# Where the table of x's remainders is made in VectorE's octet: two operations in a row, or one in each of two places

## The chip, the cores and the metric

The kernel runs on one core of a Trainium2 chip. The metric is the device time of one execution in microseconds; of several runs the median is given. The core has five engines with instruction streams of their own: PE (TensorE, matmuls), DVE (VectorE), ACT (ScalarE), POOL (GpSimd) and SP (SyncE, which here only issues DMAs). They wait for each other through semaphores.

## The reference

One layer of a graph network with 12500 nodes (x: 12500 x 64) and 400000 edges, sorted by their destination, with 16 attributes each. For every edge a small network works on the rows of its two nodes and on its attributes, the messages are added up by destination, and a node's row and its sum make the new row:

```python
m_in = jnp.concatenate([x[src], x[dst], edge_attr], axis=-1)
h = jax.nn.silu(m_in @ W1 + b1)
messages = jax.nn.silu(h @ W2 + b2)
agg = jax.ops.segment_sum(messages, dst, num_segments=x.shape[0])
node_in = jnp.concatenate([x, agg], axis=-1)
out = jax.nn.silu(node_in @ W3 + b3)
x = _layernorm(x + out, axis=-1)
```

## The kernel before

**Octets.** The edges are cut into 3125 tiles of 128 and these into 391 octets of up to 8 tiles. One turn of the main loop (`for o in range(NO + 2)`) works on several octets at once: it compares the destinations of octet o + 2 (`compare_nodes`, L587), turns octet o + 1 (L605 on PE, L615 on VectorE), runs the first layer of octet o (L640, L643, L644 on PE, the activation h at L647 on ACT), the second layer of octet o - 2 (L656 and L658 on PE, the activation m at L662 on ACT), the sum of octet o - 4 (L671 on PE) and its addition into the table `agg` at octet o - 5 (`add_window`, L682 on VectorE). An h activation happens once an octet.

**Where an edge's source row comes from.** The 8 tiles are 4 pairs. Most pairs are gathered by GpSimd with an indirect DMA for each tile (L538, tile `ga`), up to octet 10 from x and from octet 11 on from `pa`, the product of x with a part of W1. These gathers stand in no order with the other engines: GpSimd goes on until the ring of five `ga` buffers is full, and then waits for the PE transposes (L640) that read the oldest. Other pairs are picked from the resident transposed x, a node's column after another: by ACT (L447, tile `cx`), by VectorE (L449, `cx`), by PE (`pick`, tile `pg`), and by single DMAs from SP (`rx`).

**Columns.** `columns(o, engine, part)` copies a share of such columns. On VectorE a part is 0 or 32 edges, 16 instructions of L449, and ahead of it stands a TENSOR_LOAD (L430) that reads the 32 addresses into registers. Part 1 is empty; part 3 is empty in three octets of seven.

**The table of remainders.** PE's pick is exact in float32 up to octet 57 (L396). From octet 58 it adds two bfloat16 products instead (L400 and L402): the upper halves of x's float32 words, and the remainders, x minus its upper halves, from the table `rest2`. `remainders(k)` makes that table on VectorE, 512 columns in four operations: k % 4 = 0 subtracts for the lower 64 partitions (L810, into `rest2`), 1 subtracts for the upper 64 (L812, into a buffer in `v`), 2 casts that buffer into `rest2` (L814), 3 subtracts the rounded value from it (L816). L814 reads what L812 wrote, and L816 what L814 wrote. There are 100 operations in all. The same memory had served before as a staging buffer for `pa` (L232 and its DMAs, up to octet 6).

**The order of the work.** Instructions of PE, ACT, VectorE and SP stand in the order in which this loop is written (`manual_schedule`). On VectorE an octet is: L682, L587, the remainders, columns part 0 (L430, L449), `window_copy` (L567), L615, columns part 2, columns part 3 where there is one, now and then node work (L732, L737, L738, L750), address arithmetic (L523), limits (L288). L615 frees the one PSUM buffer `ph` into which PE's next L605 writes, so PE's turn of octet o + 2 waits for L615 of octet o + 1.

Of the kernel before, what the change touches and what calls it, by code (L numbers as in the profile page):

```python
# [32 lines left out]
BEGIN = 4  # L33
# [29 lines left out]
def kernel(  # L63
# [51 lines left out]
    with ExitStack() as inner:  # L115
        flag = windows(inner, tc, ident, identb, twice, badi, pa, x, xt, xt2, src_c, src_row, src_pair, dst_c, dst_row, attr_t, attr_2, base, w1, b1, w2, b2, w3, b3, out, edges)
# [5 lines left out]
def windows(ctx, tc, ident, identb, twice, badi, pa, x, xt, xt2, src_c, src_row, src_pair, dst_c, dst_row, attr_t, attr_2, base, w1, b1, w2, b2, w3, b3, out, edges):  # L122
# [5 lines left out]
    NO = base.shape[1]  # L128
# [184 lines left out]
    with tc.tile_pool(name="gat", bufs=AHEAD + 2) as gat, \  # L313
# [20 lines left out]
        def shares(eng, o):  # L334
            if o < BEGIN:
                return (0, 0, 0, 0)
            if eng == ENG.Activation:
                return ACOLS if (o - BEGIN) % 7 % 3 < 2 else (ACOLS[0] - 16, ACOLS[1])
            n = (o + 1 - BEGIN) * VRATE[0] // VRATE[1] - (o - BEGIN) * VRATE[0] // VRATE[1]
            return VCOLS if n == 3 else VCOLS[:3] + (0,)  # L340
# [75 lines left out]
        def columns(o, eng, part):  # L416
            if o < BEGIN:
                return
            lo = counts[eng][o] + sum(shares(eng, o)[:part])
            hi, most = lo + shares(eng, o)[part], LOADS[eng == ENG.DVE]  # L420
            while lo < hi:
                j, e0 = lo // (2 * P), lo % (2 * P)
                if j >= len(pairs[eng]):
                    return
                n = min(hi - lo, 2 * P - e0, most)
                key = eng, pairs[eng][j]
                if key not in cols:
                    cols[key] = cx.tile([P, P], F32, name="cx")
                t = cols[key].bitcast(U8)
                _, regs = nc.values_load_multi_w_load_instructions(  # L430
                    indices[eng, j][0:1, e0:e0 + n], engines=(eng,), min_val=XADDR,
                    max_val=X2ADDR + 4 * (N - 1), skip_runtime_bounds_check_because="src names a node")

                def at(i, u, a):
                    return u[:, ds(regs[i].with_bounds(min_val=a, max_val=a + 4 * (N - 1)) - a, 4)]

                def word(i, u, a):
                    o = (regs[i] - a).with_bounds(min_val=0, max_val=4 * (N - 1), guaranteed_mod_val=0, out_of_modulus=4)
                    return u[:, ds(o, 4)].bitcast(F32)

                for i in range(n):
                    e = e0 + i
                    if e % 8 >= 4:
                        continue
                    k = e // 8 * 4 + e % 4
                    if eng == ENG.Activation:
                        nc.scalar.activation(cols[key][:, k:k + 1], word(i, xb, XADDR), AF.Identity, bias=word(i + 4, x2b, X2ADDR))  # L447
                    else:
                        nc.vector.tensor_tensor(t[:, 4 * k:4 * k + 4], at(i, xb, XADDR), at(i + 4, x2b, X2ADDR), op=OP.max)  # L449
                lo += n  # L450
# [109 lines left out]
        def window_product(o):  # L560
            pw = mis.tile([P, P], F32, name="mm")
            nc.tensor.matmul(pw[:E, :], winrow[o], w1bb.rearrange("k s m -> k (s m)"),  # L562
                             start=True, stop=True)
            winrow[o] = pw

        def window_copy(o):
            nc.vector.tensor_tensor(xw[o % 3][:E, :], winrow.pop(o)[:E, :], mask[:E, :], op=OP.mult)  # L567
# [11 lines left out]
        def compare_nodes(o):  # L579
            c, t0, n, first, last = octs[o]  # L580
            eh = ehp.tile([P, OT // 2, S, 2], F32, name="eh")
            rel = dcs[t0 // SCT].bitcast(F32)
            t0 = t0 % SCT

            def compare(i, k, s, w):
                at = t0 + 2 * i + s
                nc.vector.tensor_tensor(eh[:, i:i + k, :, s:s + w], row[:, None, :, None].to_broadcast([P, k, S, w]),  # L587
                                        rel[:, at:at + k * w].rearrange("p (i s) -> p i s", s=w)[:, :, None, :].to_broadcast([P, k, S, w]),
                                        op=OP.is_equal)

            k = n // 2
            compare(0, k, 0, 2)
            if n % 2:
                compare(k, 1, 0, 1)
                nc.vector.memset(eh[:, k, :, 1], 0.0)
            hots[o] = [eh]
# [12 lines left out]
        def turned(o):  # L609
            c, t0, n, first, last = octs[o]  # L610
            eh, ph = hots[o]
            e = o % 3 * OT // 2 * P
            w = (n + n % 2) // 2 * P
            oh = loaded[c][:, e:e + w]
            nc.vector.tensor_copy(oh[:E, :], ph[:E, :(n + 1) // 2].rearrange("p i e -> p (i e)"))  # L615
            hots[o] = oh, eh
# [155 lines left out]
        for q in range(rest):  # L772
            o = lead[due[q]] + LAST - 1
# [11 lines left out]
        for q0, q1 in batches:  # L785
            o = lead[due[q1 - 1]] + LAST + 2 * G
# [10 lines left out]
        def remainders(k):  # L797

            c = k // 4 * RW
            if c >= N:  # L800
                return
            w = min(RW, N - c)
            at = slice(c, c + w)

            def top(t):
                return t.bitcast(BF16).rearrange("p (n s) -> p n s", s=2)[:, at, 1]

            left = v[D:, 2 * RB - 2:].rearrange("p a i d -> p (a i d)")[:, :w]
            if k % 4 == 0:
                nc.vector.tensor_tensor(rest2[:D, at], xs[:D, at], top(xs)[:D], op=OP.subtract)  # L810
            elif k % 4 == 1:
                nc.vector.tensor_tensor(left, x2[D:, at], top(x2)[D:], op=OP.subtract)  # L812
            elif k % 4 == 2:
                nc.vector.tensor_copy(rest2[D:, at], left)  # L814
            else:
                nc.vector.tensor_tensor(rest2[D:, at], left, rest2[D:, at], op=OP.subtract)  # L816
# [52 lines left out]
        with tc.manual_schedule(engines={ENG.PE, ENG.Activation, ENG.DVE, ENG.SP}):  # L869
# [8 lines left out]
            for o in range(NO + 2):  # L878
# [50 lines left out]
                        nc.vector.memset(t[:, c:min(c + XC, w)], 0.0)  # L929
                if o + 2 < NO:  # L930
                    compare_nodes(o + 2)
                for k in (2 * (o - BEGIN - 5), 2 * (o - BEGIN - 5) + 1) if o >= BEGIN + 5 else ():
                    remainders(k)
                columns(o, ENG.DVE, 0)
                def behind():
                    for q in adds.get(o, []):
# [18 lines left out]
                if o + 1 < NO:  # L955
                    if o + 1 < NO - 1:
                        window_copy(o + 1)
                    if o + 1 == NO - 2:
                        window_product(o + 2)
                        window_copy(o + 2)  # L960
                    columns(o, ENG.DVE, 1)
                    turned(o + 1)
                    columns(o, ENG.DVE, 2)
                columns(o, ENG.DVE, 3)
                if phase == 20:
# [317 lines left out]
```

## Time and profile before

| | |
|---|---|
| median of 3 runs | 3247.89 us (3245.48 to 3252.06) |
| the profiled execution, its own time | 3249.99 us |
| its span | 3248.0 us |
| busy: PE / DVE / ACT / POOL | 2642.2 / 2119.8 / 3084.4 / 2425.1 us |
| gathers from pa (L538) | 2459, 953 ns each in the mean |
| remainders: L810, L812, L814, L816 | 25 each, median 671, 689, 425, 690 ns |
| first and last start of a remainder | 128.8 and 564.1 us |

The span runs from the first to the last instruction of the profiled execution; its own time has the start and the end around it. In groups of instructions, a line names the source line, engine, operation, output and inputs; behind the bar stand busy time, the mean of one in ns, and the engine's idle time just before them with what ended it. "issue" is time in which an engine waited for nothing that the profile shows. A row with "<-" between two instructions is a wait: who waited for whom, us in total, how often, and the longest. A window's row has the engines' busy times PE, PEld (weight loads), DVE, ACT, POOL with instruction counts, then the granted TensorE clock, the DMA share and GB/s. Rows of a timeline have start, duration, and in brackets the idle time before.

### The profile page before, as it was taken

What the parts mean: (1) busy time and instruction counts of PE and PEld (TensorE: products, weight loads), DVE (VectorE), ACT (ScalarE), POOL (GpSimd) and SP (SyncE); (2) the same over time, 40 slices, a digit from 0 to 9 for tenths busy, and PEclk for the clock granted to TensorE, in tenths of its full rate; (3) what the DMA queues carried; (4) which work ended last, traced back from release to release, by engine and by line L of the source; (5) the groups of instructions that cost most, each with busy time, mean ns of one, the idle gap of its engine ahead of it and who ended that gap; (6) DMA issues with size and microseconds to landing.
All of it is one profiled execution on the core that took longest, in us unless ns stands there. A gap on an engine that the chain in (4) does not pass through costs nothing. (4 is left out here: it accounts for less than half of the span.)

```text
span 3248.0 us, 124643 instructions
## 1 busy us (share of the span) xinstructions
PE 2642.2 (81%) x32267; PEld 2170.6 (67%) x32267; DVE 2119.8 (65%) x18208; ACT 3084.4 (95%) x15185; POOL 2425.1 (75%) x2551
## 2 busy tenths in 40 slices
PE   7788778788787887887888888878888778888776
PEld 5677667676676766666666667667666666666664
DVE  5577777666666666666666666666666666666663
ACT  2799988999999999999999999999999999999994
POOL 7777776777777777777777777777777777777775
PEclk8787877787777777878877777877778788777887
DMA  7211111221221221222221222222221221222211
GB/s 148 49 41 40 40 39 37 43 48 42 43 43 41 49 43 43 43 46 44 43 44 41 46 43 43 43 43 46 43 44 41 45 46 42 44 43 45 44 41 36
DMA packets 157997, 148.42 MB, mean 46 GB/s; under 512 B 101606, under 2 KB 111604, under 8 KB 156516
## 3 DMA queue, kind: packets, MB, share of 16 engines
q0 software_dynamic: 81376, 83.49, 13.5%
q1 hardware_dynamic: 61406, 47.11, 5.6%
q10 hardware_dynamic: 14502, 9.75, 1.4%
q8 instruction: 272, 4.46, 0.6%
q14 instruction: 441, 3.61, 0.4%
HBM read 133.72 MB, written 6.40 MB: 43 GB/s over the span
## 5 line engine op out<-in xcount | busy, mean ns | idle before, releaser
L538 POOL DMA_INDIRECT ga<-pa,sc x2459 | 2344.6, 953 | 772.0 <-issue 661.0
L447 ACT ACTIVATE cx<-xs,x 128x1 f32 x14336 | 2829.6, 412 | 18.8 <-issue 14.8
L449 DVE TENSOR_TENSOR cx<-xs,x 128x4 uint8 x15616 | 1261.1, 155 | 1009.4 <-issue 989.8
L658 PEld LDWEIGHTS p<-w2d,h 128*128 128x128 f32 x3126 | 512.7, 233 | 245.9 <-issue 227.9
L402 PEld LDWEIGHTS <-twice 128*128 128x128 bf16 x7680 | 434.8, 100 | 265.5 <-issue 257.2
L400 PEld LDWEIGHTS <-twice 128*128 128x128 bf16 x7680 | 469.6, 100 | 124.6 <-issue 124.6
L644 PE MATMUL p<-oh,xw 128*128 128x512 f32 x760 | 545.9, 811 | 0.0
L400 PE MATMUL pg<-xs,twice 128*128 x7680 | 478.5, 165 | 69.5 <-DVE px L414 35.6
L658 PE MATMUL p<-w2d,h 128*128 128x128 f32 x3126 | 514.5, 319 | 0.0
L402 PE MATMUL pg<-rest,twice 128*128 x7680 | 468.0, 164 | 1.6 <-DVE rest L816 1.6
L605 PE MATMUL ph<-identb,eh 128*96 128x128 bf16 x1563 | 206.6, 271 | 243.2 <-DVE oh L615 237.2
L656 PE MATMUL p<-b2r,one 128*128 128x512 bf16 x391 | 172.6, 441 | 232.3 <-ACT m L662 231.3
L605 PEld LDWEIGHTS <-eh 128*96 128x96 bf16 x1563 | 150.5, 159 | 264.2 <-DVE oh L615 256.1
L647 ACT ACTIVATE h<-p 128x512 f32<-128x512 f32 x391 | 275.4, 704 | 52.6 <-PE p L644 27.1
L662 ACT ACTIVATE m<-p 128x512 f32<-128x512 f32 x391 | 276.0, 706 | 36.7 <-PE p L658 33.5
L671 PE MATMUL pg<-eh,m 128*64 128x48 f32 x6250 | 307.2, 245 | 0.7 <-ACT m L662 0.7
L640 PE MATMUL p<-ident,ga 128*128 128x128 f32 x1230 | 268.5, 344 | 10.6 <-DMA ga<-pa,sc 10.6
L671 PEld LDWEIGHTS pg<-eh,m 128*64 128x64 f32 x6250 | 255.7, 158 | 22.7 <-issue 13.3
L615 DVE COPY oh<-ph 96x512 f32<-96x512 f32 x391 | 263.3, 673 | 2.2 <-PE ph L605 2.1
L587 DVE TENSOR_TENSOR eh<-wrow,dc 128x384 f32<-128x384 f32 x392 | 213.3, 544 | 10.7 <-ACT z L726 6.1
L562 PE MATMUL mm<-w1bb,xr 66*96 66x128 f32 x782 | 214.8, 367 | 0.8 <-ACT rest L232 0.7
L640 PEld LDWEIGHTS p<-ident,ga 128*128 128x128 f32 x1230 | 206.1, 184 | 12.1 <-issue 12.1
(127 smaller groups left out, 1846.8 us busy)
## 6 DMA issues: line engine op xcount, KB each, us to landing
rx<-pa SPq DMA_DIRECT2D x6144, 0.2 KB
ga<-pa,sc POOLq DMA_INDIRECT x2459
oh<-in_attr SPq DMA_DIRECT2D x130, 192.0 KB
xr<-in_xt SPq DMA_DIRECT2D x391, 24.4 KB
cxi<-in_src_pair SPq DMA_DIRECT2D x234, 1.0 KB
xs<-in_xt ACTq DMA_DIRECT2D x6, 512.0 KB
pa<-rest ACTq DMA_DIRECT2D x12, 256.0 KB
x<-in_xt ACTq DMA_DIRECT2D x6, 512.0 KB
```

What stands on the lines that cost most here:

```text
L400: nc.tensor.matmul(g[:, s, k:k + 1], twice, xs.bitcast(U8)[:, ds(top, 2)].bitcast(BF16), start=True, stop=False, skip_group_check=True)
L402: nc.tensor.matmul(g[:, s, k:k + 1], twice, rest2.bitcast(U8)[:, ds(at, 2)].bitcast(BF16), start=False, stop=True, skip_group_check=True)
L447: nc.scalar.activation(cols[key][:, k:k + 1], word(i, xb, XADDR), AF.Identity, bias=word(i + 4, x2b, X2ADDR))
L449: nc.vector.tensor_tensor(t[:, 4 * k:4 * k + 4], at(i, xb, XADDR), at(i + 4, x2b, X2ADDR), op=OP.max)
L538: nc.gpsimd.indirect_dma_start(out=ga[:, i, :], out_offset=None, in_=x if o < RAW else pa[:, :], in_offset=bass.IndirectOffsetOnAxis(ap=sc ...
L605: nc.tensor.matmul(ph[:E, i, :], eh[:, i, :, 1], identb, start=(i == 0), stop=(i == k - 1), skip_group_check=True)
L640: nc.tensor.matmul(p1[:, i, :], g2.rearrange("p s d -> p (s d)"), ident, is_transpose=True, start=(i == c), stop=False, skip_group_check=True)
L644: nc.tensor.matmul(p1[:, :k], xw[o % 3], oh, start=False, stop=True, skip_group_check=True)
L647: nc.scalar.activation(h[:, :k], p1[:, :k], AF.Silu)
L658: nc.tensor.matmul(p2[:, 2 * i:2 * i + 2, :].rearrange("p s d -> p (s d)"), h[:, i, :], w2d, start=False, stop=(i == k - 1), skip_group_ch ...
L662: nc.scalar.activation(m[:, :n2], p2[:, :n2], AF.Silu)
L671: nc.tensor.matmul(pg[s * D:(s + 1) * D, :], m[:, i, :], eh[:, i // 2, :, s], start=(i < 2), stop=(i >= n - 2), skip_group_check=True)
```

## The change

Before, octets 9 to 58 each make two remainders one behind the other, ahead of columns part 0. Now octets 8 to 57 each make two, the first at that same place and the second behind L615, ahead of columns part 2. The operations, their number and their order among themselves are the same; the table is complete one octet earlier.

```diff
                 if o + 2 < NO:
                     compare_nodes(o + 2)
-                for k in (2 * (o - BEGIN - 5), 2 * (o - BEGIN - 5) + 1) if o >= BEGIN + 5 else ():
-                    remainders(k)
+                spread = 2 * (o - BEGIN - 4) if BEGIN + 4 <= o < NO else None
+                if spread is not None:
+                    remainders(spread)
                 columns(o, ENG.DVE, 0)
...
                     columns(o, ENG.DVE, 1)
                     turned(o + 1)
+                    if spread is not None:
+                        remainders(spread + 1)
                     columns(o, ENG.DVE, 2)
                 columns(o, ENG.DVE, 3)
```

BEGIN is 4. VectorE in octet 13 before (rest_102 is the table `rest2`, TENSOR_LOAD reads register values, x16 stands for 16 instructions):

```order
L682 TENSOR_TENSOR agg<-agg,pg_246 128x48
L587 TENSOR_TENSOR eh<-wrow,dc 128x384
L810 TENSOR_TENSOR rest_102<-xs 64x512
L812 TENSOR_TENSOR v<-x 64x512
L430 TENSOR_LOAD cxi
L449 TENSOR_TENSOR cx<-xs,x_104 128x4 x16
L567 TENSOR_TENSOR xw_187<-mm,mask 96x128
L615 COPY oh<-ph 96x512
L430 TENSOR_LOAD cxi
L449 TENSOR_TENSOR cx<-xs,x_104 128x4 x16
```

Both remainders of the octet stand between L587 and the first TENSOR_LOAD. VectorE at the start of octet 14 before, behind that:

```order
L682 TENSOR_TENSOR agg<-agg,pg_247 128x48
L587 TENSOR_TENSOR eh<-wrow,dc 128x384
L814 CAST rest_102<-v 64x512
L816 TENSOR_TENSOR rest_102<-v,rest_102 64x512
L430 TENSOR_LOAD cxi
L449 TENSOR_TENSOR cx<-xs,x_104 128x4 x16
```

The other two of the four operations stand in the same place, L816 right behind L814, whose output it reads. VectorE in octet 13 now:

```order
L682 TENSOR_TENSOR agg<-agg,pg_246 128x48
L587 TENSOR_TENSOR eh<-wrow,dc 128x384
L814 CAST rest_102<-v 64x512
L430 TENSOR_LOAD cxi
L449 TENSOR_TENSOR cx<-xs,x_104 128x4 x16
L567 TENSOR_TENSOR xw_187<-mm,mask 96x128
L615 COPY oh<-ph 96x512
L816 TENSOR_TENSOR rest_102<-v,rest_102 64x512
L430 TENSOR_LOAD cxi
L449 TENSOR_TENSOR cx<-xs,x_104 128x4 x16
L682 TENSOR_TENSOR agg<-agg,pg_247 128x48
```

L816 has moved behind the column copies and L615, and stands ahead of the second TENSOR_LOAD; in the octets around it L810 and L812 stand in the same two places. The rows of PE, ACT, GpSimd and SP are in the order that they had.

## The prediction

> **What bounds the kernel now.** I read the end first, then who waits for whom, then the stretch in which the moved operations stand. The chain that ended last (start us, us, what) runs back through GpSimd's gathers:
>
> ```profile
> 3209.57 2.20 DMA ga<-pa,sc
> ...
> 3217.08 0.94 POOL ga L538
> 3218.02 0.30 issue
> 3218.33 2.35 DMA ga<-pa,sc
> 3220.81 0.45 PE p L640
> ```
>
> So the end is set by when GpSimd issues its last gathers. The groups of GpSimd's instructions, asked for in three stretches (112 to 565 us, 565 to 1000, 1000 to 3226), show how it got there; behind the bars stand busy time, mean ns of one, and idle time before them with its releasers:
>
> ```profile
> L538 POOL DMA_INDIRECT ga<-pa,sc x342 | 331.4, 969 | 123.0 <-issue 91.2 <-PE p L640 19.5 <-DMA ga<-pa,sc 7.0
> L538 POOL DMA_INDIRECT ga<-pa,sc x346 | 328.7, 950 | 107.3 <-issue 92.5 <-DMA ga<-pa,sc 8.3 <-PE p L640 2.9
> L538 POOL DMA_INDIRECT ga<-pa,sc x1772 | 1685.3, 951 | 540.8 <-issue 477.9 <-DMA ga<-pa,sc 42.7 <-PE p L640 5.8
> ```
>
> In the last stretch the idle time is 540.8 / 1772 = 0.305 us a gather, which is the cost of issuing one: GpSimd never waits from 1000 us on. Held against that, the second stretch has 107.3 - 346 x 0.305 = 1.8 us too much and the first 123.0 - 342 x 0.305 = 18.7 us, and it is PE's transposes (L640) that end it: the five ga buffers are full and the gather waits until the main loop has used the oldest. These 20.5 us are all the slack in the engine that sets the end.
>
> Why is the main loop slow there? Busy time of the engines in two stretches of 420 us, the h activations (one an octet) in each, and the waits of ACT and PE in the first of them:
>
> ```profile
> 145.00:565.00 420.00, 350.25 (x3413) 291.09 (x3413) 301.64 (x2317) 386.58 (x1905) 305.19 (x316) 0.80 0.19 40
> 565.00:985.00 420.00, 343.93 (x4537) 282.63 (x4535) 274.71 (x2476) 418.66 (x2079) 316.70 (x334) 0.77 0.21 44
> ```
>
> ```profile
> L647 ACT ACTIVATE h<-p 128x512 f32<-128x512 f32 x48 | 28.3, 589 | 8.3 <-PE p L644 6.7 <-PE p L635 1.6
> L647 ACT ACTIVATE h<-p 128x512 f32<-128x512 f32 x52 | 35.6, 684 | 0.1
> ```
>
> ```profile
> ACT m L662 <- PE p L658: 16.1, 9, 2.5
> PE ph L605 <- DVE oh L615: 61.8, 26, 5.3
> ```
>
> ```profile
> PE ph L605 <- DVE oh L615: 50.5, 24, 5.4
> ```
>
> (The last row is PE's in the second stretch.) The first stretch, where the remainders stand, takes 420 / 48 = 8.75 us an octet, the second 420 / 52 = 8.08 with ACT busy all but 1.3 us. In the first ACT is idle for 420 - 386.6 = 33.4 us; it waits for PE, and PE for VectorE's copy of the one-hots (L615). One such wait and what follows it on PE:
>
> ```profile
> 515.39 0.66 PE L605 MATMUL ph<-identb,eh 128*96 128x128 bf16 x4 [4.09 <-DVE oh L615]
> ...
> 519.24 3.47 PE L396 MATMUL pg<-xs,ident 128*64 x31
> ...
> 528.64 1.97 PE L396 MATMUL pg<-xs,ident 128*64 x31
> ```
>
> After an idle of 4.09 us the same 31 matmuls took 3.47 us, an octet later 1.97: a late L615 costs more than its lateness. So the order in this stretch is VectorE, then PE, then ACT; and GpSimd, ahead of all of them, stands in front of full buffers.
>
> **The change part by part.** It removes and adds nothing: 100 remainder operations in octets 9 to 58 become 100 in octets 8 to 57, one ahead of columns part 0 and one behind L615, ahead of part 2. VectorE in two neighbouring octets before, L810 and L812 in the first, L814 and L816 in the second:
>
> ```profile
> 305.62 0.19 DVE L682 TENSOR_TENSOR agg<-agg,pg 128x48 f32 x1
> 305.74 0.55 DVE L587 TENSOR_TENSOR eh<-wrow,dc 128x384 f32<-128x384 f32 x1
> 306.21 0.68 DVE L810 TENSOR_TENSOR rest<-xs 64x512 bf16<-64x512 f32 x1
> 306.91 0.69 DVE L812 TENSOR_TENSOR v<-x 64x512 f32<-64x512 f32 x1
> 307.63 1.29 DVE L449 TENSOR_TENSOR cx<-xs,x 128x4 uint8 x16
> ...
> 309.05 0.67 DVE L615 COPY oh<-ph 96x512 f32<-96x512 f32 x1
> 310.38 1.27 DVE L449 TENSOR_TENSOR cx<-xs,x 128x4 uint8 x16 [0.66 <-issue]
> ...
> 311.91 0.18 DVE L682 TENSOR_TENSOR agg<-agg,pg 128x48 f32 x1
> ...
> 312.60 0.42 DVE L814 CAST rest<-v 64x512 bf16<-64x512 f32 x1
> 313.06 0.69 DVE L816 TENSOR_TENSOR rest<-v,rest 64x512 bf16<-64x512 f32 x1
> 315.26 1.33 DVE L449 TENSOR_TENSOR cx<-xs,x 128x4 uint8 x16 [1.51 <-issue]
> ...
> 316.71 0.67 DVE L615 COPY oh<-ph 96x512 f32<-96x512 f32 x1
> ```
>
> And in an octet without remainders, later, with the load of register values that stands ahead of each group of column copies:
>
> ```profile
> 598.81 0.17 DVE L682 TENSOR_TENSOR agg<-agg,pg 128x48 f32 x1
> ...
> 600.92 1.27 DVE L449 TENSOR_TENSOR cx<-xs,x 128x4 uint8 x16 [1.47 <-issue]
> ...
> 602.31 0.67 DVE L615 COPY oh<-ph 96x512 f32<-96x512 f32 x1
> 603.72 1.26 DVE L449 TENSOR_TENSOR cx<-xs,x 128x4 uint8 x16 [0.74 <-issue]
> ```
>
> ```profile
> L430 DVEq TENSOR_LOAD <-cxi x976: 2095/2100/2790, 64.5 to 3173.7; - x196
> ```
>
> The load takes 2.10 us. At 307.63 the copies start 0.03 us after L812 ends, so their load was under way beside the operations ahead of it: VectorE's sequencer runs ahead of its operations, unless one of them has to wait. L816 reads what L814 writes and waits for it, so the load behind L816 goes out only as L816 starts, and the copies 2.20 us after that (313.06 to 315.26), 1.51 of them idle. Behind L812, which waits for nothing unfinished, the load is already done.
>
> *Front, from L682 to the end of L615.* Before: 309.05 + 0.67 - 305.62 = 4.10 us in the first octet, 316.71 + 0.67 - 311.91 = 5.47 in the second. In the new order neither kind has a self-wait ahead of the load: L814 reads what L812 wrote an octet earlier, L816 what L814 wrote some 2 us earlier. Upper bound: the load goes out only at L682, as in the octet without remainders, whose idle 1.47 us covers the one remainder of 0.42 to 0.68: 602.31 + 0.67 - 598.81 = 4.17, so 0.07 lost in the one and 1.30 gained in the other. Lower bound: the load is always early and the operations alone count: 4.10 - 0.69 = 3.41, and 5.47 - 0.69 - 1.51 = 3.27, a gain of 0.69 and 2.20. A pair of octets gains 1.23 to 2.89 us here. I take 1.4, near the upper bound of the time, since bn_stats and bn_aggr (the second waits for the first) stand ahead of L682 in most octets from the 30th on and make the load late there.
>
> *Behind L615.* The second remainder (0.69; L812 or L816) falls into the idle 0.66 to 0.74 us ahead of the next column copies, in which the register load is under way. Covered, it costs up to 0.06 us an octet; uncovered (without that idle time) 0.69 + 0.03. I take 0.05: the load's issue does not depend on it. A pair then gains 1.3, with bounds of 1.23 - 1.44 = -0.2 and 2.9.
>
> *The main loop.* 25 pairs make 25 x 1.3 = 32 us of VectorE's time; the bounds are -5 and +72. ACT's idle 33.4 us is the most that the loop can return, so octets of 8.1 to 8.2 us instead of 8.75, about 28 us over 50 of them.
>
> *The end.* In the first stretch GpSimd needs 316 / 48 = 6.6 gathers of 0.969 + 0.305 us an octet, 8.4 us, more than the loop then takes. So the loop no longer holds GpSimd back, its 20.5 us of waits go, and nothing beyond them: after that it issues without a pause to the end, as it does now. Of the loop's 28 us some 8 are lost to a smaller lead of the gathers over their use. What follows the last gather keeps its length. The profiled execution took 3249.99 us with a span of 3248.0; 3249.99 - 20.5 = 3229.5. The median of the runs, 3247.89, lies 2.1 below it: 3227.4. I predict 3228.
>
> [...] Gathers near the remainders:
>
> ```profile
> 306.11 0.95 POOL L538 DMA_INDIRECT ga<-pa,sc  x1 [0.30 <-issue]
> 307.36 1.06 POOL L538 DMA_INDIRECT ga<-pa,sc  x1 [0.31 <-issue]
> ```
>
> The one that began under L812 took 0.11 us longer, the one that began ahead of L810 no longer; over the stretch the mean is 969 ns against 951. Spread out, 50 more gathers could begin under a remainder: 50 x 0.11 = 5.5 us at most. [...]
>
> **The rivals.** *VectorE stays late (3236).* If half of the second remainder is uncovered, a pair gains 1.3 - 0.7 = 0.6 and the loop 15 us; GpSimd's waits shrink by what the loop gains, the end by 10 to 15. For it: VectorE has as much to do in the octet as the loop has time (8.1), and a load that is late by a little shows at once. Against it: the gap behind L615 is there in every octet shown. Chance 0.18.
>
> *No change (3247).* PE's slow octets feed on themselves (3.47 against 1.97 us) and keep ACT and the ga buffers waiting though L615 comes earlier. For it: PE waits 4.09 us, and 1.3 us a pair closes only part of that. Against it: after 565 us the loop holds 8.08 although PE waits 24 times for L615, up to 5.4 us. Chance 0.08.
>
> *Slower (3295).* The load ahead of columns part 2 cannot pass the second remainder, as it now cannot pass L816: the copies then begin 2.20 us after the remainder does, 2.23 after L615, not 0.70. That is 1.53 an octet against a front gain of at least 0.6: 50 x 0.93 = 47 us on the loop, and since GpSimd is waiting for the loop already, on the end. It decides as soon as the load is late by more than 0.6 us in the mean. For it: L816 keeps a wait on VectorE itself. Against it: its producer L814 is now some 2 us old, and L812 with a wait on an older operation let the load pass. Chance 0.05.
>
> *Gathers held in full (3262).* Each of 50 more gathers loses 0.69 us: 34.5 against the 20.5 won, 14 slower. The rows show a sixth of it (0.11). Chance 0.02. [...]
>
> **How the numbers follow.** The forecast has 0.67. Its own range is 3222 to 3233: down by the 342 x 0.018 = 6 us which the gathers lose beside remainders now, up by the 5.5 above. With most of the first rival the range is 3222 to 3240, and 0.2 or less lies outside. A measurement of this kernel tells about 0.2%, 6.5 us, from no change. Faster by more than that: 0.67 + 0.18 - 0.01 = 0.84; within it 0.09; slower 0.07.
>
> **What would show it.** L449's idle time before it in 145 to 565 us falls, and rows with L816 just ahead of L449 show no gap near 1.5. The h activations in that stretch rise from 48 to 51 or 52, and ACT's idle time falls from 33 us to below 12. GpSimd's idle time ended by L640 in the first stretch falls from 19.5 to what a normal issue leaves (below 4), and its last gather starts some 20 us earlier than 3224.6, with as much time behind it. I am wrong if a gap of 1.5 us stands behind L615's remainder, if GpSimd still waits for L640 there, or if the loop gains 25 us and the end does not move.

## The result, and the profile after

| | before | after |
|---|---|---|
| median of 6 runs each | 3246.67 us (3243.02 to 3252.06) | 3227.92 us (3225.65 to 3232.97) |
| ratio | | 0.9945, 95% interval 0.9932 to 0.9958 |
| the profiled execution, its own time | 3249.99 us | 3226.88 us |
| its span | 3248.0 us | 3224.9 us |
| h activation of octet 58 / 383 / 390 starts at | 565.2 / 3178.3 / 3231.5 us | 531.9 / 3153.1 / 3208.7 us |

The kernel became 0.55% faster by that ratio, 18.8 us in the medians and 23.1 us between the two profiled executions. GpSimd's gathers in the three stretches of the prediction (112 to 565 us, 565 to 1000, 1000 to 3226), now:

```profile
L538 POOL DMA_INDIRECT ga<-pa,sc x352 | 346.2, 984 | 109.8 <-issue 94.0 <-DMA ga<-pa,sc 7.9 <-DMA xr<-in_xt 2.7
L538 POOL DMA_INDIRECT ga<-pa,sc x347 | 329.3, 949 | 105.9 <-issue 93.6 <-DMA ga<-pa,sc 8.8 <-PE p L640 1.5
L538 POOL DMA_INDIRECT ga<-pa,sc x1760 | 1668.5, 948 | 536.8 <-issue 471.8 <-DMA ga<-pa,sc 43.3 <-PE p L658 7.3
```

In the first, the idle time is within 109.8 - 352 x 0.305 = 2.4 us of what issuing costs, where it was 18.7 over; and these 2.4 us stand ahead of the very first of these gathers, in a gap of 2.7 us that a window load (`xr`) ended. What L640 ends in that stretch, 19.5 us before, is now four ordinary issues of 0.3 us:

```profile
POOL ga L538 <- PE p L640: 1.2, 4, 0.3
```

Between the first and the last of the 2459 gathers GpSimd was idle for 770.5 us before and is now for 749.7, which is 0.305 each: no wait for a full ring is left. The first and last start of these gathers, from the view of that line (min, median and max ns, first and last start):

```profile
L538 POOL DMA_INDIRECT ga<-pa,sc x2459: 940/944/1642, 111.5 to 3204.3; - x190
```

The last one started at 3224.6 before: 20.3 us earlier now. From it to the span's end are 20.6 us, against 23.4. The main loop in the two stretches of 420 us, then its h activations and waits in the first of them:

```profile
145.00:565.00 420.00, 353.27 (x3810) 297.71 (x3809) 323.60 (x2515) 415.41 (x2072) 320.53 (x326) 0.85 0.20 41
565.00:985.00 420.00, 335.22 (x4508) 274.86 (x4509) 277.40 (x2483) 419.88 (x2075) 317.90 (x335) 0.81 0.20 44
```

```profile
L647 ACT ACTIVATE h<-p 128x512 f32<-128x512 f32 x53 | 33.3, 629 | 0.0
```

```profile
PE ph L605 <- DVE oh L615: 37.6, 19, 4.2
PE p L656 <- ACT m L662: 26.0, 15, 2.9
ACT m L662 <- PE p L658: 2.8, 2, 2.6
```

53 octets where there were 48, and ACT idle for 4.6 us instead of 33.4. PE still waits for L615, 19 times instead of 26, but ACT hardly waits for PE, and PE now waits for ACT: ACT's own work sets the pace, as after 565 us. VectorE in two neighbouring octets of the new order, L810 and L812 in the first, L814 and L816 in the second:

```profile
321.40 0.20 DVE L682 TENSOR_TENSOR agg<-agg,pg 128x48 f32 x1 [0.27 <-issue]
...
321.99 0.67 DVE L810 TENSOR_TENSOR rest<-xs 64x512 bf16<-64x512 f32 x1
323.77 1.27 DVE L449 TENSOR_TENSOR cx<-xs,x 128x4 uint8 x16 [1.11 <-issue]
...
325.16 0.67 DVE L615 COPY oh<-ph 96x512 f32<-96x512 f32 x1
325.87 0.69 DVE L812 TENSOR_TENSOR v<-x 64x512 f32<-64x512 f32 x1
326.60 0.16 DVE L449 TENSOR_TENSOR cx<-xs,x 128x4 uint8 x1
...
328.80 0.17 DVE L682 TENSOR_TENSOR agg<-agg,pg 128x48 f32 x1
...
329.47 0.42 DVE L814 CAST rest<-v 64x512 bf16<-64x512 f32 x1
330.92 1.28 DVE L449 TENSOR_TENSOR cx<-xs,x 128x4 uint8 x16 [1.02 <-issue]
...
332.32 0.67 DVE L615 COPY oh<-ph 96x512 f32<-96x512 f32 x1
333.02 0.69 DVE L816 TENSOR_TENSOR rest<-v,rest 64x512 bf16<-64x512 f32 x1
333.76 1.30 DVE L449 TENSOR_TENSOR cx<-xs,x 128x4 uint8 x16
```

Behind L615 the remainder fills the gap in which the load of register values runs, and the copies follow it at once (333.02 + 0.69 = 333.71, then 333.76). Ahead of part 0 there is still a gap, but L814 and L816 together no longer stand in front of it. In the two rows shown it is 1.0 to 1.1 us; over the 25 octets of each kind it is 0.69 us in the mean with L810 (0.08 before) and 0.55 with L814 (1.53 before). All octets from 12 to 56, in the mean, worked out from the starts and ends of the same rows ("front" is from L682's start to L615's end; "behind" from L615's end to the next copies; a bar stands for L615's place):

| octet with | front | behind | octet |
|---|---|---|---|
| before: L810, L812, bar (22 octets) | 4.13 | 0.71 | 7.99 |
| before: L814, L816, bar (23) | 5.54 | 0.78 | 9.72 |
| after: L810, bar, L812 (23) | 4.18 | 0.83 | 8.42 |
| after: L814, bar, L816 (22) | 3.89 | 0.81 | 7.86 |

The L810 octet gained nothing, the L814 octet 1.65 us at the front. A pair of octets takes 16.28 us instead of 17.71. The load itself shows why: in all 25 octets with L814 and L816 it started 0.01 to 0.08 us after L816 did before, and in the change it starts 0.9 to 1.5 us before L816.

The loop's gain is 33.3 us at octet 58 but 25.2 at octet 383. What takes the rest back shows in the waits of PE for gathered tiles between 532 and 3153 us, first before, then after:

```profile
PE p L640 <- DMA ga<-pa,sc: 1.3, 1, 1.3
```

```profile
PE p L640 <- DMA ga<-pa,sc: 158.4, 123, 3.0
```

The loop now runs ahead of the gathers and waits for them from octet to octet.

### The profile page after: what moved, and what is told of

The parts are those of the page before. It is cut to its first block, busy times and chain, and to the rows that moved or that the text cites. A ratio compares the mean times of both kernels' runs of the same rounds, so it can differ in the third digit from the quotient of the medians.

```text
span 3224.9 us, 124642 instructions
## 1 busy us (share of the span) xinstructions
PE 2653.5 (82%) x32267; PEld 2147.8 (67%) x32267; DVE 2121.8 (66%) x18208; ACT 3081.6 (96%) x15185; POOL 2424.3 (75%) x2551
## 5 line engine op out<-in xcount | busy, mean ns | idle before, releaser
L538 POOL DMA_INDIRECT ga<-pa,sc x2459 | 2344.0, 953 | 752.4 <-issue 659.4
L447 ACT ACTIVATE cx<-xs,x 128x1 f32 x14336 | 2790.1, 360 | 15.1 <-issue 11.2
L658 PEld LDWEIGHTS p<-w2d,h 128*128 128x128 f32 x3126 | 528.8, 240 | 136.6 <-issue 117.5
L658 PE MATMUL p<-w2d,h 128*128 128x128 f32 x3126 | 528.0, 325 | 0.0
L640 PE MATMUL p<-ident,ga 128*128 128x128 f32 x1230 | 286.2, 335 | 171.9 <-DMA ga<-pa,sc 170.9
L605 PE MATMUL ph<-identb,eh 128*96 128x128 bf16 x1563 | 197.1, 262 | 177.7 <-DVE oh L615 172.4
L640 PEld LDWEIGHTS p<-ident,ga 128*128 128x128 f32 x1230 | 196.6, 174 | 206.8 <-issue 175.3
L671 PE MATMUL pg<-eh,m 128*64 128x48 f32 x6250 | 320.5, 252 | 0.7 <-ACT m L662 0.7
L647 ACT ACTIVATE h<-p 128x512 f32<-128x512 f32 x391 | 255.3, 653 | 47.9 <-PE p L644 24.9
L671 PEld LDWEIGHTS pg<-eh,m 128*64 128x64 f32 x6250 | 268.0, 165 | 23.3 <-issue 15.9
L662 ACT ACTIVATE m<-p 128x512 f32<-128x512 f32 x391 | 255.2, 653 | 23.6 <-PE p L658 21.0
L615 DVE COPY oh<-ph 96x512 f32<-96x512 f32 x391 | 263.2, 673 | 3.0 <-PE ph L605 2.9
L587 DVE TENSOR_TENSOR eh<-wrow,dc 128x384 f32<-128x384 f32 x392 | 213.2, 544 | 11.0 <-PE wrow L714 5.8
L562 PE MATMUL mm<-w1bb,xr 66*96 66x128 f32 x782 | 202.9, 350 | 0.8 <-ACT rest L232 0.7
```

Of the source, the lines that this page charges most:

```text
L538: nc.gpsimd.indirect_dma_start(out=ga[:, i, :], out_offset=None, in_=x if o < RAW else pa[:, :], in_offset=bass.IndirectOffsetOnAxis(ap=sc ...
L605: nc.tensor.matmul(ph[:E, i, :], eh[:, i, :, 1], identb, start=(i == 0), stop=(i == k - 1), skip_group_check=True)
L640: nc.tensor.matmul(p1[:, i, :], g2.rearrange("p s d -> p (s d)"), ident, is_transpose=True, start=(i == c), stop=False, skip_group_check=True)
L647: nc.scalar.activation(h[:, :k], p1[:, :k], AF.Silu)
L658: nc.tensor.matmul(p2[:, 2 * i:2 * i + 2, :].rearrange("p s d -> p (s d)"), h[:, i, :], w2d, start=False, stop=(i == k - 1), skip_group_ch ...
L671: nc.tensor.matmul(pg[s * D:(s + 1) * D, :], m[:, i, :], eh[:, i // 2, :, s], start=(i < 2), stop=(i >= n - 2), skip_group_check=True)
```

## Experiments

The kernels ran in three groups, each on one chip together with the kernel before, and the ratios are those on record against it there (they can differ by some 0.0005 from the quotient of the medians). First group (before: 3245.2 us, 16 runs): the change again, the register load first, both remainders behind L615, no remainders. Second group (3251.64 us, 21 runs): the two that split one pair, and both kernels with fewer gathers. Third group (3242.1 us, 16 runs): the change once more, the kernel before with fewer gathers once more, and more rows by SP.

### The change, again

No edit: the changed kernel itself, for the ratio in the first and the third group.

> The changed kernel again, beside the others on one chip, to compare them with. 3226 to 3230 us, 17 to 20 us below the kernel before on the same chip; 52 or 53 h activations in 145 to 565 us and no wait of GpSimd for L640 there.

> The changed kernel again, beside the three others of this job. 0.994 of the kernel before, GpSimd's last gather some 20 us ahead of the end.

Measured: 3226.56 us, 0.9942 (0.9928 to 0.9956), and 3226.78 us, 0.9958 (0.9944 to 0.9972). Fronts and octets of the two are within 0.12 us of the table above.

### The register load ahead of both remainders

If the gain comes from the load of register values getting out early, then in the order before it should suffice to put the load ahead of the two remainders:

```diff
+                if between:
+                    between()
+                    between = None
...
-                for k in (2 * (o - BEGIN - 5), 2 * (o - BEGIN - 5) + 1) if o >= BEGIN + 5 else ():
-                    remainders(k)
-                columns(o, ENG.DVE, 0)
+                def both():
+                    for k in (2 * (o - BEGIN - 5), 2 * (o - BEGIN - 5) + 1) if o >= BEGIN + 5 else ():
+                        remainders(k)
+                columns(o, ENG.DVE, 0, both)
```

The first three lines stand in `columns`, behind the load and ahead of the copies.

> Both remainders stay where they were, ahead of L615, in octets 9 to 58; only the load of register values for columns part 0 stands ahead of them and not behind. Theory of the exposed load: L816's wait for L814 hurt because the load stood behind it. In the octet of L810 and L812 nothing changes (4.10 us from L682 to the end of L615), in that of L814 and L816 5.47 falls to about 4.1, 1.4 us a pair and so the whole of the gain I gave to the change: 51 or 52 h activations in 145 to 565 us, no waits of GpSimd for L640 above 3 us in all, 3226 to 3232 us. Rival, one remainder less ahead of L615 is what counts (0.69 us an octet): here none is taken away, so the octets stay near 8.7 us and the time at 3240 to 3247.

Measured: 3253.78 us, 1.0027 (1.0016 to 1.0038): slower. The expectation was wrong. VectorE's timeline (line numbers are three higher: L590 is `compare_nodes`, L813 to L819 the remainders, L452 the column copies):

```profile
308.49 0.54 DVE L590 TENSOR_TENSOR eh<-wrow,dc 128x384 f32<-128x384 f32 x1
310.02 0.68 DVE L813 TENSOR_TENSOR rest<-xs 64x512 bf16<-64x512 f32 x1 [0.99 <-issue]
310.73 0.69 DVE L815 TENSOR_TENSOR v<-x 64x512 f32<-64x512 f32 x1
311.45 1.29 DVE L452 TENSOR_TENSOR cx<-xs,x 128x4 uint8 x16
...
317.23 0.42 DVE L817 CAST rest<-v 64x512 bf16<-64x512 f32 x1 [0.77 <-DVE eh L590]
317.69 0.69 DVE L819 TENSOR_TENSOR rest<-v,rest 64x512 bf16<-64x512 f32 x1
318.39 1.32 DVE L452 TENSOR_TENSOR cx<-xs,x 128x4 uint8 x16
```

The gap did not vanish; it moved to the front of the remainders, although these need no register, and the copies follow them without one. In this trace the 25 L813 and the 25 L817 start 0.09 us (median) after the load ahead of them has ended. So in this trace nothing behind the load starts until the load is done, and only operations that stand *ahead* of it cover it. The L814 octet gains (front 5.21 us against 5.54), but the L810 octet, whose load had been covered by the remainders, loses (5.02 against 4.13), and the pair takes 18.12 us. At 308.49 + 0.54 the engine was free, and L813 began 0.99 us later.

### Both remainders behind L615

Nothing ahead of part 0, and both remainders where the change puts the second:

```diff
-                for k in (2 * (o - BEGIN - 5), 2 * (o - BEGIN - 5) + 1) if o >= BEGIN + 5 else ():
-                    remainders(k)
                 columns(o, ENG.DVE, 0)
...
                     turned(o + 1)
+                    for k in (2 * (o - BEGIN - 4), 2 * (o - BEGIN - 4) + 1) if o >= BEGIN + 4 else ():
+                        remainders(k)
                     columns(o, ENG.DVE, 2)
```

> Both remainders stand behind L615, ahead of columns part 2, in octets 8 to 57. Theory of the exposed load: the front falls to 3.4 to 4.2 us in both kinds of octet, but behind L615 L810 and L812 need 1.4 us where 0.7 is idle (0.7 lost) and L814 and L816 hold the load until L816 starts, so the copies begin 2.7 us after L615 and not 0.7 (2.0 lost). A pair changes by -1.3 to -2.9 + 2.7, that is by -0.2 to +1.4 us: the loop stays at 8.6 to 9.1 us an octet, 3240 to 3265 us, and a gap near 1.5 us stands ahead of part 2. Rival, an early L615 is what counts: L615 comes earlier than in the changed kernel, so the time is 3224 to 3230.

Measured: 3253.85 us, 1.0026 (1.0016 to 1.0035), as expected. Two octets of VectorE:

```profile
302.23 0.67 DVE L615 COPY oh<-ph 96x512 f32<-96x512 f32 x1
302.82 0.67 DVE L810 TENSOR_TENSOR rest<-xs 64x512 bf16<-64x512 f32 x1
303.53 0.69 DVE L812 TENSOR_TENSOR v<-x 64x512 f32<-64x512 f32 x1
304.25 1.28 DVE L449 TENSOR_TENSOR cx<-xs,x 128x4 uint8 x16
...
311.16 0.67 DVE L615 COPY oh<-ph 96x512 f32<-96x512 f32 x1
311.86 0.42 DVE L814 CAST rest<-v 64x512 bf16<-64x512 f32 x1
312.32 0.69 DVE L816 TENSOR_TENSOR rest<-v,rest 64x512 bf16<-64x512 f32 x1
314.53 1.26 DVE L449 TENSOR_TENSOR cx<-xs,x 128x4 uint8 x16 [1.52 <-issue]
```

The self-wait works in the same way in the other place: behind L816 the copies are 1.52 us late, 2.72 behind L615 in the mean; behind L812 they follow at once, 1.32 behind L615. The octets take 9.51 and 8.58 us. The place behind L615 is therefore not what made the change good; what counts is that L816 does not stand right behind L814.

### One pair split, the other together

Split only the pair that waits for itself (L814 | L816), and L810 and L812 both ahead:

```diff
-                for k in (2 * (o - BEGIN - 5), 2 * (o - BEGIN - 5) + 1) if o >= BEGIN + 5 else ():
-                    remainders(k)
+                spread = 2 * (o - BEGIN - 4) if BEGIN + 4 <= o < NO else None
+                if spread is not None:
+                    remainders(spread)
+                    if spread % 4 == 0:
+                        remainders(spread + 1)
...
+                    if spread is not None and spread % 4 == 2:
+                        remainders(spread + 1)
```

> The change in half of the octets: L814 ahead of columns part 0 and L816 behind L615, but L810 and L812 both ahead of part 0 as before (octets 8 to 57). Theory after the first runs: a load of register values runs beside what stands ahead of it, and everything behind it waits; L816's wait for L814 keeps the load from running beside it. This kernel takes that wait away and leaves the cover of L810 and L812: octets of about 8.0 and 7.8 us from L682 to L682 instead of 8.0 and 9.7, a pair at 15.8 and so below the changed kernel's 16.3. The loop is then ACT's, GpSimd does not wait: 3225 to 3231 us, as the changed kernel. Rival, each remainder taken from ahead of L615 counts alike (0.7 us): half of the gain, 3234 to 3238 us.

Measured: 3231.8 us, 0.9939 (0.9926 to 0.9953): by the ratio the gain of the whole change, 0.8 us above the range. The shorter pair of 15.8 us did not come: it takes 16.44, close to the 2 x 8.11 of the octets without any remainder below, so something other than VectorE sets the pace there. And the opposite (0 and 2 exchanged): L810 | L812 split, L814 and L816 together.

> The other half of the change: L810 ahead of part 0 and L812 behind L615, but L814 and L816 both ahead of part 0 as before (octets 8 to 57). Theory: the wait of L816 and the idle 1.5 us behind it stay, and taking L812 away from ahead of the load uncovers the load; octets of 8.1 to 8.5 and 9.6 us, a pair at 17.7 to 18.1: no gain, 3241 to 3250 us, GpSimd waits 15 us and more for the ga buffers. Rival, each remainder counts alike: half of the gain, 3234 to 3238 us.

Measured: 3249.19 us, 0.9994 (0.9985 to 1.0003). GpSimd's gathers from 112 to 565 us, with L814 | L816 split and then with L810 | L812 split:

```profile
L538 POOL DMA_INDIRECT ga<-pa,sc x355 | 346.4, 976 | 108.3 <-issue 95.2 <-DMA ga<-pa,sc 8.6 <-PE p L640 1.5
```

```profile
L538 POOL DMA_INDIRECT ga<-pa,sc x343 | 333.6, 973 | 119.8 <-issue 92.4 <-PE p L640 17.6 <-DMA ga<-pa,sc 7.0
```

The one has the whole gain and no waits, the other no gain and the waits of before. Of the 25 octet pairs that the change touches, only the L814 octets matter for the gain. Fronts and octets:

| kernel | L810 octet: front, octet | L814 octet: front, octet |
|---|---|---|
| before | 4.13, 7.99 | 5.54, 9.72 |
| only L814, L816 split | 4.37, 8.52 | 3.93, 7.92 |
| only L810, L812 split | 4.06, 8.27 | 5.50, 9.40 |
| the change | 4.18, 8.42 | 3.89, 7.86 |

### No remainders at all

The table is filled with zeros in 16 octets, and nothing is computed for it; so the picked rows from octet 58 on lack what the lower halves of x's words add:

```diff
-                for k in (2 * (o - BEGIN - 5), 2 * (o - BEGIN - 5) + 1) if o >= BEGIN + 5 else ():
-                    remainders(k)
+                if BEGIN + 5 <= o < BEGIN + 21:
+                    nc.vector.memset(rest2[:, (o - BEGIN - 5) * 782:min((o - BEGIN - 4) * 782, N)], 0.0)
```

> The remainders are left out (the table is set to zero by 16 short memsets in octets 9 to 24), so the lower halves of the columns picked by PE are missing from the result. Theory that GpSimd's gathers set the end now: the loop cannot move the end any more, and only what the remainders cost the gathers comes back: in the changed kernel 91 gathers beside a remainder took 1.07 us, the others 0.95; 352 x (0.984 - 0.951) = 11 us. 3214 to 3220 us, no waits of GpSimd for L640. Rival, VectorE still sets the end through the remainders it keeps (a pair's 2.5 us): 25 x 1.3 = 32 us less than the changed kernel, 3196 us. Rival, remainders do not hold gathers: 3227 us.

Measured: 3220.22 us, 0.9923 (0.9909 to 0.9936), 6 us below the change in the same group (whose interval, 0.9928 to 0.9956, overlaps) and just above the expected range. Its windows row and gathers, in the stretches shown for the others:

```profile
145.00:565.00 420.00, 361.60 (x3779) 305.86 (x3777) 273.80 (x2443) 414.55 (x2068) 318.10 (x335) 0.83 0.20 42
```

```profile
L538 POOL DMA_INDIRECT ga<-pa,sc x361 | 343.4, 951 | 110.1 <-issue 97.0 <-DMA ga<-pa,sc 8.8 <-PE mm L562 0.9
```

VectorE is busy 50 us less than with the change, and ACT no busier (414.55 us against 415.41): with the change VectorE has stopped being the limit, and the octets here take 8.11 us against 8.14. What is left of the remainders' price is in the gathers of this stretch: 951 ns each against 973 in the changed kernel of this group, and 355 x 0.022 = 7.8 us. How much of that reaches the end is open: over the whole run the 2459 gathers took 2338.8 us against 2342.6, and of the 7.5 us by which the last one starts earlier (3195.7 and 3203.2) the first one, ahead of any remainder, already had 3.8 (108.2 and 112.0).

### Fewer gathers

Does GpSimd set the end, so that the loop's 33 us cannot all arrive? From octet 100 on every fourth octet leaves out the gathers of its last two tiles, and its transposes read the tiles before them; 140 gathers fewer (2319 instead of 2459), and those tiles have other edges' rows.

```diff
+        def spared(o):
+            return o >= 100 and o % 4 == 0 and octs[o][2] == OT and len(slots[o]) + (o in rpairs) < OT // 2 - 1
...
-                if i // 2 < len(slots[o]) + (o in rpairs):
+                if i // 2 < len(slots[o]) + (o in rpairs) or spared(o) and i >= n - 2:
                     continue
...
```

The kernel before, so edited:

> The kernel before with fewer gathers: from octet 100 on every fourth octet leaves out its last two (some 140 of 2459, 175 us of GpSimd's time) and uses another pair's rows in their place, so those messages are wrong. GpSimd then cannot set the end. Theory: the loop is ACT's up to octet 383 as before (start at 3178 us), and only the last seven octets no longer wait for gathers: 3222 to 3242 us. It is the kernel to hold the next one against.

The changed kernel, so edited:

> The changed kernel with the same gathers left out. Theory that the change gave the loop 33 us (octet 58's h at 531.9 us instead of 565.2) and that GpSimd let only 20 of them reach the end: against the kernel before with the same gathers left out it is 29 to 34 us faster. Rival, the loop's gain is given back elsewhere and not to GpSimd: 18 to 23 us, as with all gathers.

Measured: 3252.25 us, 1.0003 (0.9994 to 1.0013), for the kernel before, and 3217.92 us, 0.9896 (0.9881 to 0.9911), for the changed one. Between the medians the change is worth 34.3 us where gathers are fewer, not 18.8, as if the loop's whole gain arrived; whether the two can be held against each other follows below. But fewer gathers alone gave nothing, against the expectation of 3222 to 3242, while the one profiled execution took 3228.76 us and the ten others 3249.72 to 3254.17. So it was run again in the third group:

> The kernel before with fewer gathers once more (from octet 100 on every fourth octet leaves out its last two, and their messages are wrong). Its first execution took 3228.8 us and ten others 3250 to 3254; in the profiles of that job ACT took 186 ns from one column to the next in three kernels and 185 in this one. If ACT's rate decides whether the loop or GpSimd sets the end of the kernel before: where the kernel before takes about 3246, this one takes 3228 to 3240; where the kernel before takes 3251, this one takes 3251 too. Rival, the first execution was a stray one: as the kernel before in either case.

Measured: 3234.32 us, 0.998 (0.9971 to 0.9989), from 3232.21 to 3237.21 in 11 runs: 7.8 us less than before. The traces tell how these fit. From the h activation of octet 383 to that of 390 the loop takes 53.2 us in the kernel before, 37.2 and 37.5 in its two profiles with fewer gathers; so there the last gathers came some 16 us late. In the profile of the kernel with only L810 | L812 split, from the second group, the same stretch takes 37.9 us with all gathers: the loop itself was slower, because a column step on ACT (L447, median of the distances between starts) took 186 ns where the profiles of the other groups have 185. 14336 such steps are 14 us. So in the kernel before, loop and gathers end within some 16 us of each other, and in these profiles a nanosecond of ACT's step decides which is last. That the ten unprofiled runs had the slower step is inferred, not shown, and the 34.3 us are a comparison of like with like only if they had, since the changed kernel with fewer gathers was profiled at 186 ns. Between the two profiles with fewer gathers of the second group, the kernel before and the changed one, octet 58 starts 26.2 us earlier (559.2 and 533.0), neither waits at the end (37.5 and 38.2 us from octet 383 to 390), and only the slower step takes time back between: 2628.6 us against 2613.7 from octet 58 to 383. So in these two profiles nothing but the gathers, and the step, stands between the loop's gain and the end. Two such kernels at the same step were not measured.

### More rows by SP

If gathers are the limit, hand some to SP's single row DMAs: the changed kernel with 27 pairs' rows by SP (6 gathers fewer), and with 29 (10 fewer).

```diff
-ROWS = (220, 13)
+ROWS = (240, 13)
```

> The changed kernel with more pairs fetched row by row by SP: 240 rows in 13 octets and not 220, 27 pairs and not 24, so 6 gathers fewer for GpSimd (7.5 us at 1.25). Theory that GpSimd's gathers set the end of the changed kernel and the loop has some 8 us in hand (33 us gained up to octet 58, 25 left at octet 383): 5 to 7 us below the changed kernel, 0.992 of the kernel before. Rival, ACT's loop sets the end now: the same as the changed kernel within 2 us.

> The same with 260 rows in 13 octets: 29 pairs, 10 gathers fewer (12.5 us), SP busy with 20 rows of about 0.34 us an octet, 6.8 of 8.05 us. Theory: 8 to 11 us below the changed kernel, since the loop has no more than about 8 in hand and a little in its last octets; 0.991 of the kernel before. Rivals: the same as the changed kernel (ACT), or slower than it because SP comes too late with its rows or with the tiles that it loads behind them.

Measured: 3359.28 us, 1.0368 (1.035 to 1.0387), and, with 260, 3579.78 us, 1.1036 (1.1017 to 1.1055). Far slower, against the theory in both; the expectation for 260 had named this as a rival, SP coming too late with the tiles that it loads behind the rows. Waits for the windows of x (`xr`) that SP loads in the same queue, first with 240, then with 260:

```profile
PE mm L562 <- DMA xr<-in_xt: 441.3, 216, 5.3
```

```profile
PE mm L562 <- DMA xr<-in_xt: 652.1, 267, 6.0
```

In the changed kernel no wait of PE for them shows.

The octets from 58 to 383 take (3291.5 - 531.6) / 325 = 8.49 us with 240 / 13 = 18.46 rows an octet, and (3522.0 - 560.9) / 325 = 9.11 with 20: 0.46 us a row, all in. From 600 to 2600 us SP issued a row every 0.477 us in the changed kernel, every 0.460 with 240 and every 0.456 with 260, so more rows hardly went out any faster. With 220 / 13 = 16.9 rows 0.46 us each is 7.8 us of an octet of 8.06: by this estimate SP had hardly any time left before. No kernel that does the whole computation was clearly faster than the change.

## Why the prediction was right, point by point

The forecast of 3228 us stood against 3227.92. That the two agree to 0.1 us is luck: six runs of the change spread over 7 us, and the sum started from a median of 3247.89 us that became 3246.67 with three further runs. That the end came some 20 us earlier, and why, is not. By the forecast's own steps:

**What bounds the kernel: right for the loop, partly for the end.** VectorE was late, through PE, to ACT: with L814 and L816 apart ACT's idle time fell from 33.4 to 4.6 us (below 12 was said), and the octets counted in that stretch rose to 53 (51 or 52 were said). So neither the rival in which VectorE stays late nor the one in which nothing changes came about. The prediction saw that a late L615 costs PE more than its lateness, but not in what: the 31 matmuls of L396 took 1.97 us at a granted TensorE clock of 1.0 and 3.47 at 0.5. From 145 us on, 10 of 48 such blocks took over 3 us before, and 2 of 47 after. That the gathers alone set the end held for the profile that was read; the runs with fewer gathers show that freeing them brings nothing to 7.8 us, since the loop ends right behind. The sum did not suffer: both had to become earlier by 20 us, and both did.

**Front, 1.4 us a pair: right in sum, wrong in its parts.** 1.60 was measured (4.13 + 5.54 - 4.18 - 3.89). The upper bound of the time (0.07 lost in the L810 octet, 1.30 gained in the other) was the right picture: 0.05 lost, 1.65 gained. The reason given for staying near that bound was right in kind but counted too often: bn_stats and bn_aggr stand at the end of octets 30 to 33 and 45 to 48, and so ahead of L682 in 8 of the 28 octets from the 30th to the 57th, not in most. In the 8 octets behind them the idle time ahead of part 0 is 1.0 us in the mean, in the other L814 octets 0.63 up to the 29th and 0.28 from the 30th on; so the gain went past 1.30. The gain in the L810 octet that the other bound allowed, 0.69, never came: the remainder that left had covered the load, and the idle time ahead of part 0 grew by 0.61 us (0.08 to 0.69). The two runs that split one pair show it: all of the gain in one, none in the other.

**Why the load is late: the wait was right, the picture of the load was too simple.** In the 25 octets with L810 and L812 before, the load started 0.46 to 1.82 us ahead of L810, which stands in front of it; in those with L814 and L816 it started 0.01 to 0.08 us after L816. So L816's wait on L814 does hold the load back, in either place (1.51 us idle ahead of part 0, 1.52 behind L615). But "their load was under way beside the operations ahead of it" is only half of it: the operations behind the load wait too (0.99 and 0.77 us in the two rows with the load first). The run with the load first fell for that reason.

**Behind L615, 0.05 an octet: 0.075 measured.** The means are 0.83 and 0.81 us, against 0.71 and 0.78, so 0.15 a pair where 0.10 stood. The cover was there, as said. The rival in which the load passes the second remainder late (3295) is a real mechanism, seen with both remainders behind L615, but needs L814 directly ahead of L816.

**The loop, 28 us: 33.3.** A pair gains 1.43 us instead of 1.3, and 25 of them make 36. The octets were said to become 8.1 to 8.2 us: the mean of the two kinds is 8.14.

**The end, 20.5 us: right.** The idle time between the first and the last gather fell by 20.8 us (770.5 to 749.7). Their busy time stayed the same (2344.6 and 2344.0 us) and the first one started 1.0 later, so the last one started 20.3 us earlier. What follows it was to keep its length and became 2.8 us shorter; no run tells why. "Some 8 lost to a smaller lead": 33.3 - 25.2 = 8.1. The end of the loop waits 2.4 us more (octet 383 to 390: 55.6 us against 53.2), and 33.3 - 8.1 - 2.4 = 22.8 of the span's 23.1.

**Gathers beside remainders, 5.5 us at most: 2 to 6, but spread otherwise.** In the first stretch 70 gathers overlapped a remainder by more than 0.2 us before, of 1.03 us against 0.95 for the others, and 93 of 1.07 after (96 of 1.03 and 96 of 1.04 in the other two profiles of the change). Together they lost 5.3 us before and 11.0 after (7.2 and 8.6). But the prediction read its row of 1.06 us wrongly when it took the 0.11 us that this gather lost for the most that one can lose. That gather began at 307.36, when L812 had only 0.24 us to go (306.91 + 0.69 = 307.60), and it ended 0.82 us after L812 did. One that begins earlier under a remainder loses more, as here after the change:

```profile
349.26 0.69 DVE L816 TENSOR_TENSOR rest<-v,rest 64x512 bf16<-64x512 f32 x1
```

```profile
349.34 1.43 POOL L538 DMA_INDIRECT ga<-pa,sc  x1 [0.30 <-issue]
```

It too ends 0.82 us after the remainder (350.77 and 349.95). Of the gathers that began while a remainder had more than 0.2 us to go, 22 of 28 before and 31 of 33 after ended 0.80 to 0.84 us after it, whatever was left of it. So in these two profiles such a gather mostly stood still until the remainder had ended. The mean loss is small because most of the 70 began ahead of the remainder, where few were held (8 of 42 took over 1.00 us), and the others lost only what was left of it. The rival of 3262 failed not for want of a hold, but because the change put hardly more gathers under a remainder: 49 began there (37 and 41 in the other two profiles) against 45 before, where it counted 50 more. The loss was not seen at the end, because the gathers from 1000 us on took 948 ns instead of 951, 5 us over 1760, for a reason that no run here tells.

## What to carry to other kernels

Look for two neighbouring operations of which the second reads the first's result, with a register load behind them: here the second's wait kept the load from going out (it started 0.01 to 0.08 us after the second did, and took 2.10), and the load kept everything behind it from starting (1.53 us idle in the mean). Put such operations apart, and leave queued work without a wait of its own ahead of each load; splitting the pair that had no such wait gained nothing here. And before counting a stage's gain, look at what runs in no order with it: the loop won 33 us, but the gathers had only 20 of waits to give.

## What was not expected of the hardware

A register load of 2.10 us on VectorE was covered by queued work ahead of it (0.08 us idle behind it with L810 and L812 before) and by nothing behind it: operations without any use of its registers stood still for 0.99 and 0.77 us behind it in the rows shown. SP issued its row DMAs every 0.46 us in the mean with 240 and with 260 rows in 13 octets, against 0.477 in the changed kernel, and one and a half rows more an octet (16.9 to 18.5) delayed the window loads behind them enough for 4% of the time. Of the 61 gathers in the two profiles that began under a remainder with more than 0.2 us to go, 53 ended 0.82 us after it, whatever was left of it. A column step on ACT took 185 ns in all other profiles, and 186 in three of the four of the second group; over 14336 steps that is 14 us, three quarters of what the change brought.
